# Windowed attention in a four-layer kernel: the softmax quotient moved to VectorE, one more gather issued by ScalarE, a shorter root and a bias sum placed by hand

## The chip, the core and the metric

The kernel runs on one core of a Trainium2 chip. A core has five engines with instruction streams of their own: TensorE (PE: matrix products into the accumulator memory PSUM; its weight loads are listed apart as PEld), VectorE (DVE), ScalarE (ACT), GpSimd (POOL) and SyncE (SP, which here issues transfers only). The metric is the time of the whole program on the device in microseconds. Three runs of the kernel before gave a median of 3369.8 us (3368.98 to 3379.31).

## The reference

The input is a batch of 8 images of 128 channels, 56 x 56 pixels, in fp32. Four residual layers follow one another, each on a group norm of its input (`x = x + layer(_gn(x))`). The change is in layer 0, attention between windows; one line of layer 1 moves.

```python
# layer 0, per image: 7 x 7 windows of 8 x 8 pixels, 8 heads of 16 channels
proj = xw @ W_qkv + b_qkv                      # queries, keys, values
logit = einsum('npc,nqc->npq', mean(q) * SCALE, mean(k))
topk_logit, r_idx = top_k(logit, 4)            # each window picks 4 windows
k_sel, v_sel = kv_pix[r_idx]                   # 256 keys and values a window
attn = softmax(einsum('bmqc,bmkc->bmqk', q_h * SCALE, k_sel))
o = einsum('bmqk,bmkc->bmqc', attn, v_sel)
out = (o + lepe) @ W_o + b_o                   # lepe: 3x3 depthwise of the values
```

Group norm takes `1 / sqrt(var + eps)` per group. Layer 1 is a recurrence over the 3136 pixels of an image, `h = tanh(xgate + h @ w_hh.T)`, where `xgate` has the two biases `b_ih + b_hh` added. Layers 2 and 3 are 3x3 convolutions.

## The kernel before

Layer 0 works on pairs of windows: 8 images of 49 windows make 196 pairs (`END`). A loop over p from -3 to END + 5 writes the order of TensorE, ScalarE, VectorE and GpSimd out by hand (`manual_schedule`); each engine executes its instructions in the order in which this loop emits them. SP's instructions are put into its queue in the order of their issue as well. In one turn, each step is a different stage of a different pair:

- `scores(p + 2)` (L534): queries times keys, 16 products into the four PSUM banks s0 to s3; `maxima` (L541, VectorE): the negated maxima of each bank; `halve` (L547, L548, GpSimd) splits them into two bf16 parts; `flip` (L553, TensorE) turns them; `flipped` (L557, ScalarE) copies them to SBUF as `nm`.
- `shifted(p + 1)`: four products of ones with `nm` start the banks t0 to t3 (L566), and 32 products of keys with queries are added (L576); `exponentials` (L586, ScalarE, one per bank) read them.
- `values(p)` (L600): 64 products of the gathered value pixels with the exponentials, into one bank `po`. The pixels carry columns of ones, so `po` holds for each group of 16 channels also the divisor of the softmax. TensorE first waits for the semaphores `landed`, which count the arrival of the pixels.
- then, for pair p: `divisors` (VectorE: a transpose of `po`, L622, which reads the whole bank; reciprocals of its divisors, L628; a transpose that spreads them back, L630), `first_heads` (ScalarE, L610: the even heads of `po` times a mask), `both_heads` (VectorE, L615: the odd heads added) and `divide` (GpSimd, L648: numerator times reciprocal, written into the strip `o` of a row of windows in image order).
- `join` (L437, GpSimd) adds `o` to the depthwise result `lep`; `project` multiplies by W_o, and VectorE adds it into X (L450).

Into the turns a planner places further jobs: for each strip of seven windows queries, keys, image, pixels, depthwise convolution and projection, and for each image the norm's statistics and the routing. A job has a TensorE part and an "end", the instruction that reads the PSUM result. Each turn has up to three jobs, `one`, `two` and `light`. The order of a turn is one of two strings, SHORT or LONGER (with a depthwise job, or with `two` alone). PSUM is shared by a table of slots: `values` uses bank s0 again, `one` t0, `two` t1, `flip` t2. So the next score product into s0 has to wait until all readers of `po` are done, and the next ones product into t1 until the end of `two` is. In SHORT the end of `two` comes last in the turn; it is on ScalarE except for projections. VectorE's own loose work (normalising, window sums, statistics) goes where a running `weight` per turn is smallest; the norm's ends and the routing aren't counted in that weight.

`fetch` (L515) issues the gathers of value pixels, two windows a turn and four transfers of 32 KB each: seven by SP and the first of each pair by ScalarE, all into a ring of six windows. The index of each comes from a register that `loaded` (L470) fills from the routing table in SBUF: SP for four windows at a time, ScalarE for every other window of seven.

For each image after the first, `var_end` takes the reciprocal root without ScalarE's table: a first value by integer arithmetic (L248 to L250) and three Newton steps of four VectorE instructions (L254 to L257). For layer 1, `bg = b_ih + b_hh` (L917) is written behind layer 0 in the program, and its place in VectorE's stream is left to the scheduler.

Of the kernel before, what the change touches and what calls it, by code (L numbers as in the profile page):

```python
# [11 lines left out]
F32 = mybir.dt.float32  # L12
# [34 lines left out]
def conv_stack_kernel(ctx: ExitStack, tc: tile.TileContext, a: dict, out: bass.AP):  # L47
# [76 lines left out]
    broken = keep.tile([1, 1], I32, name="broken")  # L124
    held = keep.tile([P, KH * (NCH - 1) * B // 16], F32, name="held")
    between = ExitStack()
    samp = between.enter_context(tc.tile_pool(name="samp", bufs=2))
    with ExitStack() as l0:
# [76 lines left out]
        def measure(b):  # L205
# [37 lines left out]
            def var_end():  # L243
# [9 lines left out]
                for _ in range(3):  # L253
                    nc.vector.tensor_tensor(t, y, y, ALU.mult)  # L254
                    nc.vector.tensor_tensor(t, t, v, ALU.mult)
                    nc.vector.tensor_scalar(t, t, -0.5, 1.5, ALU.mult, ALU.add)
                    nc.vector.tensor_tensor(y, y, t, ALU.mult)  # L257
# [175 lines left out]
        def join(b, i):  # L433

            o, t = os_.pop((b, i)), lepes[b, i]
            engine = nc.vector if (b, i) == (B - 1, NBLK - 1) else nc.gpsimd
            engine.tensor_add(t, t, o)  # L437
# [37 lines left out]
        def chosen(W, t, engine):  # L475

            if (engine, W, t) not in known:
                b, w = divmod(W, NWIN)
                if engine == mybir.EngineType.Activation:
                    at = selrs[b].rearrange("p (w t) -> p w t", t=TOPK)[:, w : min(w + 7, NWIN) : 2, t]  # L480
                    known.update(((engine, W + 2 * k, t), v) for k, v in enumerate(loaded(at, engine)))
# [25 lines left out]
        def fetch(W):  # L507

            for o in range(2):
                for t in range(TOPK):  # L510
                    h = (t % 2) * WPX
                    engine, kind = (nc.sync, mybir.EngineType.SP) if o or t else (
                        nc.scalar, mybir.EngineType.Activation)
                    at = chosen(W + o, t, kind)
                    dma = engine.dma_start(  # L515
                        ring[h : h + WPX, section(W + o, t // 2), :],
                        vpix[(W + o) // NWIN][bass.ds(at, 1)].rearrange("o x c -> (o x) c"),
                    )
                    dma.then_inc(landed[(W + o) % RING], 16)
                    tc.no_tile_sem_insts.add(dma.ins.name)  # L520
                    tc.add_to_no_dep_group(f"rows{W + o}", dma.ins)
# [66 lines left out]
        def values(p):  # L588
# [6 lines left out]
            for o in range(2):  # L595
                for h in range(2):
                    for c in range(2):
                        for g in range(4):
                            at = (section(2 * p + o, c) - h) * P + 2 * g + h
                            mm = nc.tensor.matmul(  # L600
                                po[g * CL : (g + 1) * CL, o, h], flat[:, at : at + 8 * CL - 7 : 8],
# [5 lines left out]
        def first_heads(p):  # L607

            v = pairs[p]["v"] = win.tile([P, 2, WPX], F32, name=f"v_{p}", tag="v", bufs=1)
            nc.scalar.activation(v, pairs[p]["po"][:, :, 0], AF.Identity, scale=hmask[:, 0:1])  # L610

        def both_heads(p):

            s_ = pairs[p]
            nc.vector.scalar_tensor_tensor(s_["v"], s_["po"][:, :, 1], hmask[:, 1:2], s_["v"], ALU.mult, ALU.add)  # L615

        def divisors(p):
# [3 lines left out]
            t = win.tile([P, 2, 2, 2, CL], F32, name=f"den_{p}", tag="den", bufs=1)  # L621
            nc.vector.transpose(  # L622
                t.rearrange("p o h b r -> p (o h b r)"), s_["po"].rearrange("p o h q -> p (o h q)")
            )
            at = t[:, 0, 0, 0, 16:17]
            den = bass.AP(at.tensor, at.offset, [list(at.ap[0]), [4 * CL, 2], [CL, 2], [2 * CL - 16, 2]])
            rden = win.tile([P, 2, 2, 2, 1], F32, name=f"rden_{p}", tag="rden", bufs=1)
            nc.vector.reciprocal(rden.rearrange("p o b h c -> p o b (h c)"), den)  # L628
# [5 lines left out]

        def divide(p):

            s_ = pairs.pop(p)
            for o in range(2):
                W = 2 * p + o
                b, w = divmod(W, NWIN)  # L640
# [1247 lines left out]
```

## Time and profile before

| | us |
|---|---|
| median of three runs | 3369.8 |
| the profiled execution | 3365.47 |
| its span, first to last instruction | 3363.6 |
| TensorE busy in it | 3246.4 |
| layer 0: first score product to the last value product | 29.4 to about 1187.8 |
| busy from 504 to 588 us (84 us): PE / PEld / DVE / ACT / POOL | 82.2 / 60.3 / 70.4 / 53.4 / 64.9 |
| busy from 1008 to 1092 us (84 us): PE / PEld / DVE / ACT / POOL | 77.2 / 54.3 / 56.0 / 48.6 / 59.4 |

The page gives the busy time of each engine, its course in 40 slices, the transfers, the chain of work that ended last, and the costliest groups. A row of a timeline is: start, duration, engine, line, operation, output <- inputs, shape and count, and in brackets the engine's idle time before it and what ended that. PE times are modelled in part, since products are pipelined: a TensorE that is held in the middle of a group can look busy. Engine names with a q (ACTq, SPq) are sequencer instructions such as the issue of a transfer. In the longest stretches of layer 0 a pair takes between 5.0 and 6.2 us.

### The profile page before, as it was taken

The page shows a single profiled execution, that of the slowest core. Times are in us where ns is not written, and L with a number is a line of the kernel's source. Part 1 is how long each engine was busy: PE and PEld are TensorE (multiplying, and loading weights), DVE is VectorE, ACT ScalarE, POOL GpSimd, SP SyncE. Part 2 cuts the span into 40 slices and gives each one's busy share as a digit, 9 for nine tenths or more (in the row PEclk, how much of TensorE's full clock was granted, in tenths as well). Part 3 has the DMA queues.
Part 4 walks back from the last instruction along what each step waited for, and adds up shares of the span by engine and source line. Part 5 has one row for each costly group of instructions (what it writes and reads, how often), then busy time and mean ns, then how long its engine had stood idle before and what let it go on. Part 6 is the DMA issues. An engine that isn't in the chain of part 4 may idle for free.

```text
span 3363.6 us, 103407 instructions
## 1 busy us (share of the span) xinstructions
PE 3246.4 (97%) x41152; PEld 2743.4 (82%) x41152; DVE 1767.8 (53%) x4066; ACT 1412.6 (42%) x2935; POOL 1291.8 (38%) x3797
## 2 busy tenths in 40 slices
PE   7999999999999899999999999999999999999998
PEld 5777767667676689999999999999999953489898
DVE  5888888788776732221111111111122247799999
ACT  4666666566665522222222222222211144455554
POOL 4777877877777721111111111111000046422221
PEclk9999999999999989999999999999999999999999
DMA  5455555545445411110000000000012146301001
GB/s 152 132 142 134 146 142 134 138 124 143 124 129 140 112 58 45 48 48 18 1 1 1 1 1 1 1 1 1 1 51 60 57 122 181 94 20 39 27 32 40
DMA packets 197564, 239.02 MB, mean 71 GB/s; under 512 B 42848, under 2 KB 150112, under 8 KB 197072
## 3 DMA queue, kind: packets, MB, share of 16 engines
q0 software_dynamic: 34624, 117.03, 12.7%
q1 hardware_dynamic: 145936, 108.38, 11.3%
q10 hardware_dynamic: 16512, 6.90, 0.9%
q8 instruction: 326, 5.34, 0.7%
q14 instruction: 166, 1.36, 0.1%
HBM read 133.64 MB, written 67.56 MB: 60 GB/s over the span
## 4 chain that ended last, share of the span: by engine, by line
PE 75%; DVE 18%; issue 3%; POOL 1%; ACT 1%; DMA 1%; SPq 0%; POOLq 0%; DVEq 0%; ACTq 0%
PE ps L1041 35%; PE s L534 6%; PE po L600 6%; PE po L1076 5%; PE plep L420 4%; PE pc L1267 4%; PE t L576 4%; DVE nmax L541 3%; PE pi L1016 3%; PE t L566 1%; PE pc L1275 1%; DVE u_pc3b L1632 1%; PE pq L390 1%; PE pvp L319 1%; DVE va L1499 1%
## 5 line engine op out<-in xcount | busy, mean ns | idle before, releaser
L1041 PE MATMUL ps<-hs,w_gates 128*128 128x136 f32 x7680 | 932.9, 280 | 0.4 <-issue 0.4
L1041 PEld LDWEIGHTS ps<-hs,w_gates 128*128 128x128 f32 x7680 | 911.1, 190 | 8.6 <-issue 0.5
L1064 ACT ACTIVATE hs<-ps,bg 128x136 f32<-128x136 f32 x744 | 237.9, 371 | 933.1 <-PE ps L1041 925.6
L586 ACT ACTIVATE e<-t 128x512 f32<-128x512 f32 x784 | 445.6, 595 | 345.3 <-PE t L576 273.6
L541 DVE TENSOR_REDUCE nmax<-s 128x2 f32<-128x512 f32 x784 | 487.0, 685 | 196.4 <-PE s L534 195.6
L1019 DVE SCALAR_TENSOR_TENSOR inp<-pi,bine,th 128x272 f32<-128x272 f32 x186 | 84.7, 496 | 889.2 <-ACT th L1018 889.2
L1005 POOL TENSOR_TENSOR xn<-X,ctr 128x136 f32<-128x136 f32 (+1 forms) x186 | 96.3, 536 | 876.4 <-PE pi L1016 871.6
L1041 PEld LDWEIGHTS ps<-inp,w_gates 128*128 128x128 f32 x2976 | 370.2, 190 | 13.5 <-PE pi L1016 1.1
L1041 PE MATMUL ps<-inp,w_gates 128*128 128x136 f32 x2976 | 375.4, 279 | 0.7 <-PE pi L1016 0.7
L496 POOL COPY ks<-kT 128x64 f32 x1568 | 297.0, 234 | 106.2 <-PE t L576 64.8
L600 PE MATMUL po<-e,ring 128*32 128x64 f32 x12544 | 247.2, 231 | 24.7 <-DVE nmax L541 17.9
L600 PEld LDWEIGHTS po<-e,ring 128*32 128x32 f32 x12544 | 220.0, 149 | 49.6 <-DVE nmax L541 20.1
L534 PE MATMUL s<-ks,qm 32*128 32x256 f32 x3136 | 228.4, 403 | 19.0 <-DVE v L615 15.2
L576 PE MATMUL t<-qm,ks 32*128 32x128 f32 x6272 | 235.6, 273 | 0.6 <-issue 0.6
L576 PEld LDWEIGHTS t<-qm,ks 32*128 32x128 f32 x6272 | 216.5, 188 | 4.8 <-issue 1.4
L1513 PE MATMUL pc3b<-vb,u_w2c_t 128*128 128x196 f32 x1152 | 200.9, 336 | 19.9 <-DVE vb L1494 19.9
L1513 PEld LDWEIGHTS pc3b<-vb,u_w2c_t 128*128 128x128 f32 x1152 | 197.3, 194 | 22.2 <-DVE vb L1494 22.0
L1076 PE MATMUL po<-hs,xw 128*128 128x272 f32 x744 | 203.9, 396 | 3.4
L1513 PE MATMUL pc3a<-va,u_w1c_t 128*128 128x196 f32 x1152 | 198.2, 332 | 9.1 <-DVE d_pc3a L1530 4.3
L1513 PEld LDWEIGHTS pc3a<-va,u_w1c_t 128*128 128x128 f32 x1152 | 192.9, 191 | 13.6 <-issue 10.2
L534 PEld LDWEIGHTS s<-ks,qm 32*128 32x128 f32 x3136 | 144.6, 185 | 50.1 <-DVE v L615 27.4
L1076 PEld LDWEIGHTS po<-hs,xw 128*128 128x128 f32 x744 | 132.0, 190 | 28.8 <-ACT hs L1068 9.1
(288 smaller groups left out, 4410.7 us busy)
## 6 DMA issues: line engine op xcount, KB each, us to landing
ring<-vpix SPq DMA_DIRECT2D x1372, 32.0 KB
v<-vimg POOLq DMA_DIRECT2D x56, 290.0 KB, 3.9
v<-vimg POOLq DMA_DIRECT2D x56, 289.5 KB, 4.8
v<-vimg POOLq DMA_DIRECT2D x56, 289.0 KB, 5.7
kept<-gk SPq DMA_DIRECT2D x56, 272.0 KB, 2.0
g<-kept SPq DMA_DIRECT2D x56, 272.0 KB, 2.6
xkeep<-X POOLq DMA_DIRECT2D x56, 224.0 KB, 2.5
vimg<-vrow POOLq DMA_DIRECT2D x54, 232.0 KB, 2.8
```

The lines of the kernel that those rows point to most:

```text
L420: nc.tensor.matmul(st["pl"][g * CL : (g + 1) * CL], wlep[:, dy, g, :], rows[:, g, dy : dy + WS, :HW], start=(dy == 0), stop=(dy == 2),)
L496: nc.gpsimd.tensor_copy(kw[:, t : t + 1, :], ks[b][:, bass.ds(at, 1), :])
L534: nc.tensor.matmul(s_["s"][g][:, o, :], w["qm"][h].rearrange("p h x -> p (h x)"), w["kw"][h], start=True, stop=True,)
L541: nc.vector.tensor_reduce(s_["nmax"][:, :, g], s_["s"][g], AX.X, ALU.max, negate=True)
L576: nc.tensor.matmul(s_["t"][g][:, o, c], w["kw"][h, c * P : (c + 1) * P], w["qm"][h].rearrange("p h x -> p (h x)"), start=False, stop=(o == ...
L586: nc.scalar.activation(s_["e"][g], s_["t"][g], AF.Exp)
L600: mm = nc.tensor.matmul(po[g * CL : (g + 1) * CL, o, h], flat[:, at : at + 8 * CL - 7 : 8], s_["e"][g][:, o, c, h * WPX : (h + 1) * WPX], ...
L1041: nc.tensor.matmul(ps[f][:, i], w, src, start=(i == 0 and k == 0 and h != fresh), stop=(k == KH - 1 if h else k == KI - 1 and (s < WARM or ...
L1064: nc.scalar.activation(hs[f][:, s % 2, i], ps[f][:, i], AF.Tanh, bias=bg[:, m : m + 1])
L1076: nc.tensor.matmul(po, wout[:, k, :], hs[k // 2][:, :, k % 2], start=(k == 0), stop=(k == KH - 1))
L1267: nc.tensor.matmul(pcs[n][r * CL : (r + 1) * CL], w3[:, dy, r, :], rows3[:, r, i * WS + dy : i * WS + dy + WS, :HW], start=(dy == 0), stop ...
L1513: nc.tensor.matmul(bank[:, half].rearrange("p (y x) -> p y x", x=H4), u[:, dy, k, :], v[:, k, i * RB + dy : i * RB + dy + RB, :], start=(d ...
```

## The change

The quotient is now taken between two transposes on VectorE, where the queries lie on the partitions: `turned` transposes `po`, and `divide` takes the reciprocals, multiplies numerators with them, and transposes the product into the strip `o`, which is now laid out window by window. `first_heads`, `both_heads` and GpSimd's product are gone; `join` reads `o` in the order of the image. Only `turned` reads `po`.

`fetch` takes one window. `fetch0` stands at the start of a turn, `fetch1` (the pair's second window) behind `flipped`, ahead of `lit`, the hooks, the tails and the last end. ScalarE issues the first gather of both windows, SP the other six; ScalarE's registers are loaded for eight successive windows.

The Newton steps become two instructions each (`scalar_tensor_tensor`) with one scaling at the end. The planner adds the norm's two ends, the means and the routing to the weight of the turns in which they stand. In LONGER turns the banks of `one` and `two` are exchanged. The bias sum `bg` is hooked to turn END // 2 + 10 of layer 0.

```diff
-                for _ in range(3):
-                    nc.vector.tensor_tensor(t, y, y, ALU.mult)
-                    nc.vector.tensor_tensor(t, t, v, ALU.mult)
-                    nc.vector.tensor_scalar(t, t, -0.5, 1.5, ALU.mult, ALU.add)
-                    nc.vector.tensor_tensor(y, y, t, ALU.mult)
+                for c in (3.0, 12.0, 768.0):
+                    nc.vector.scalar_tensor_tensor(t, y, v, y, ALU.mult, ALU.mult)
+                    nc.vector.scalar_tensor_tensor(y, t, -c, y, ALU.add, ALU.mult)
+                nc.vector.tensor_scalar(y, y, -1.0 / 8192, None, ALU.mult)
...
-            engine.tensor_add(t, t, o)
+            t = t.rearrange("p u (j v) -> p u j v", v=WS)
+            engine.tensor_add(t, t, o.rearrange("p j (u v) -> p u j v", v=WS))
...
-                    at = selrs[b].rearrange("p (w t) -> p w t", t=TOPK)[:, w : min(w + 7, NWIN) : 2, t]
-                    known.update(((engine, W + 2 * k, t), v) for k, v in enumerate(loaded(at, engine)))
+                    at = selrs[b].rearrange("p (w t) -> p w t", t=TOPK)[:, w : min(w + 8, NWIN), t]
+                    known.update(((engine, W + k, t), v) for k, v in enumerate(loaded(at, engine)))
...
-            for o in range(2):
-                for t in range(TOPK):
-                    h = (t % 2) * WPX
-                    engine, kind = (nc.sync, mybir.EngineType.SP) if o or t else (
-                        nc.scalar, mybir.EngineType.Activation)
+            for t in range(TOPK):
+                h = (t % 2) * WPX
+                engine, kind = (nc.sync, mybir.EngineType.SP) if t else (nc.scalar, mybir.EngineType.Activation)
...
-        def first_heads(p):
-            v = pairs[p]["v"] = win.tile([P, 2, WPX], F32, name=f"v_{p}", tag="v", bufs=1)
-            nc.scalar.activation(v, pairs[p]["po"][:, :, 0], AF.Identity, scale=hmask[:, 0:1])
-        def both_heads(p):
+        def turned(p):
             s_ = pairs[p]
-            nc.vector.scalar_tensor_tensor(s_["v"], s_["po"][:, :, 1], hmask[:, 1:2], s_["v"], ALU.mult, ALU.add)
+            t = s_["turned"] = win.tile([P, 2, 4, CL], F32, name=f"turned_{p}", tag="turned", bufs=1)
+            nc.vector.transpose(t.rearrange("p h k r -> p (h k r)"), s_["po"].rearrange("p h o q -> p (h o q)"))
...
         def divide(p):
+            t = pairs.pop(p)["turned"]
+            part, at = list(t.ap[0]), t.offset
+            den = bass.AP(t.tensor, at + 16, [part, [CL, 4], [4 * CL - 16, 2]])
+            rden = win.tile([P, 4, 2, 1], F32, name=f"rden_{p}", tag="rden", bufs=1)
+            nc.vector.reciprocal(rden.rearrange("p k h c -> p k (h c)"), den)
+            v = bass.AP(t.tensor, at, [part, [CL, 4], [4 * CL + 16, 2], [1, 16]])
+            ot = win.tile([P, 4, 2, 16], F32, name=f"ot_{p}", tag="ot", bufs=1)
+            nc.vector.tensor_tensor(ot, v, rden.broadcast_to((P, 4, 2, 16)), ALU.mult)
...
-                nc.gpsimd.tensor_tensor(
+                nc.vector.transpose(
+                    os_[b, i][:, j : j + n].rearrange("p o q -> p (o q)"),
+                    ot[:, 2 * o : 2 * o + 2 * n].rearrange("p k h r -> p (k h r)"),
                 )
...
+        for b, (name, n) in itertools.product(range(1, B), (("mean", 9), ("var", 13), ("means", 5), ("route", 10))):
+            weight[placed[name, b]] += n
...
+        hook(END // 2 + 10, lambda: nc.vector.tensor_add(bg, ih, hh))
...
-        SHORT = """fetch scores shifted gather max0 max1 values exp0 max2 exp1 max3 halve ahead one light two flip exp2
-            divisors first end1 exp3 flipped both divide lit hooks tails end2"""
-        LONGER = """fetch scores shifted gather max0 max1 values exp0 max2 exp1 max3 halve ahead two exp2 divisors first
-            flip light one exp3 flipped both divide lit hooks tails end2 end1"""
+        SHORT = """fetch0 scores shifted gather max0 max1 values exp0 max2 exp1 max3 halve ahead one light two flip exp2
+            root turned divide end1 exp3 flipped fetch1 lit hooks tails end2"""
+        LONGER = """fetch0 scores shifted gather max0 max1 values exp0 max2 exp1 max3 halve ahead two exp2 root turned
+            divide flip light one exp3 flipped fetch1 lit hooks tails end2 end1"""
...
+                    slot = dict(one="two", two="one").get(name, name) if longer else name
```

The order of TensorE's instructions is the same before and after; on ScalarE the second gather of a turn, with its register load where there is one, now stands between L557 and the last end.

## The prediction

> **What bounds the kernel now.** I read the page first. Its slices show three stages: layer 0 with its attention in the first 14 slices (to about 1190 us), layer 1's recurrence, then layers 2 and 3. TensorE is busy 97% of the span, and the change touches layer 0 and one line at layer 1's start.
>
> ```profile
> span 3363.6 us, 103407 instructions
> PE 3246.4 (97%) x41152; PEld 2743.4 (82%) x41152; DVE 1767.8 (53%) x4066; ACT 1412.6 (42%) x2935; POOL 1291.8 (38%) x3797
> ```
>
> Second, the waits between 60 and 1060 us, layer 0's steady part:
>
> ```profile
> PEld s L534 <- DVE v L615: 17.6, 48, 0.6
> ...
> PEld po L600 <- DVE nmax L541: 17.1, 9, 4.2
> ...
> PEld L566 <- issue: 39.2, 126, 0.5
> ...
> DVE bg L917 <- DMA vecs<-in_L_conv_b_hh_dram: 5.6, 1, 5.6
> ...
> PE po L600 <- DMA ring<-vpix: 4.1, 1, 4.1
> ```
>
> The reader should see three waits of TensorE on VectorE or a transfer (L534, L600), and one that names nobody: 126 pauses of up to 0.5 us before the ones-weights of L566. The timeline says who that is. One pair of windows at 401.59 us:
>
> ```profile
> 401.59 1.15 PE L534 MATMUL s<-ks,qm 32*128 32x256 f32 x16
> ...
> 401.84 0.37 ACT L557 COPY nm<-flip 128x256 bf16<-128x256 bf16 x1
> 401.92 0.48 ACTq L515 DMA_DIRECT2D ring<-vpix  x1
> 402.10 0.71 ACT L307 ACTIVATE vrow<-pvt,bqkv 128x448 f32<-128x448 f32 x1
> 402.34 0.10 PEld L566 LDWEIGHTS <-ones 2*128 2x128 bf16 x2
> ...
> 402.86 0.10 PEld L566 LDWEIGHTS <-ones 2*128 2x128 bf16 x2 [0.42 <-issue]
> ...
> 404.07 1.15 PE L600 MATMUL po<-e,ring 128*32 128x64 f32 x57
> ```
>
> ScalarE empties bank t1 (L307, "end2" of this pair's second job) until 402.81; TensorE's second ones product, which refills t1, starts at 402.86. I cut the timeline at each pair's first score product and count from there. The second ones product starts at 0.97 at the earliest (49 pairs), otherwise 0.05 behind the end of end2; values begins 1.22 later in every group: 2.19 for 0.97, 2.34 for 1.12 (59 pairs), 2.55 for 1.33 (11 pairs). So each 0.1 us that end2 slips is 0.1 us of TensorE, already now. Over the 180 pairs that matter below, the mean start is 1.12.
>
> Third, ScalarE alone at 368 us:
>
> ```profile
> 368.34 0.37 ACT L557 COPY nm<-flip 128x256 bf16<-128x256 bf16 x1 [1.07 <-PE flip L553]
> 368.61 0.64 ACT L427 ACTIVATE lep<-plep,lbv 128x448 f32<-128x448 f32 x1
> 370.34 0.48 ACTq L515 DMA_DIRECT2D ring<-vpix  x1
> 370.86 1.58 ACT L586 ACTIVATE e<-t 128x512 f32<-128x512 f32 x3 [1.62 <-PE t L576]
> ```
>
> Here a register load of 1.48 us stood before the gather's issue, and the exponential, which in other pairs starts at 2.32, started 0.04 after that issue ended, at 2.66. ScalarE's next instruction waits behind an issue.
>
> **The change, part by part** (against the profiled execution, 3365.5 us with a span of 3363.6; the median of the runs shown is 3369.8, 4.3 above).
>
> *Two gathers by ScalarE: the cost.* SP issues 6 instead of 7 per pair, each 0.65 us apart. ScalarE issues 2, and the new one (fetch1) stands behind L557 and ahead of end2; the first stays behind end2. One issue is two register steps and the 0.48 us of the row above, 0.61 together. end2 now starts about 0.27 behind the start of L557 (368.34, 368.61); with the issue between them 0.03 + 0.61 + 0.04 = 0.68 behind. L557 starts at 0.16 in an undisturbed pair, and end2 takes 0.60 to 0.71, say 0.64: it ends at 0.16 + 0.68 + 0.64 = 1.48, and TensorE's refill starts at 1.53 instead of 1.12. That is +0.41 to 0.42 in 180 pairs (the changed order has no end2 behind fetch1 in 15 of the others), 76 us. ScalarE also reads indices from SBUF once per eight windows; for odd images that load now falls on fetch1. In the changed order 24 pairs have load, issue, end2. The loads have a median of 0.92, a mean of 1.05 and a maximum of 1.82 us: 24 x 1.07 = 26 us. Sum **+102 us**. Ends: were only the 0.48 us instruction in the way, 0.28 x 180 + 24 x 0.6 = 65; did the issue wait for the copy's end as well, 0.75 x 180 + 24 x 1.5 = 171. I take 0.41, since the row at 370.86 shows exactly issue end + 0.04. Behind end2 wait the other gather's issue and the exponentials; these have till 2.7 and lose nothing further. The swap of t0 and t1 in pairs with a depthwise job changes only which ones product waits.
>
> [...]
>
> *Quotient by VectorE.* Out: transpose of po 0.45, reciprocal 0.20, transpose back 0.31, both-heads 0.31 on VectorE; 0.37 on ScalarE; 0.47 on GpSimd. In: the same transpose, reciprocal, a 128x128 product, a transpose back. The product is between a 128x1 operation (0.16) and GpSimd's neighbour row on VectorE (L1009, two 128x136 in 1.09: 0.54); nearest is both-heads of the same size, 0.31. VectorE's load stays: 766 us busy in the 960 from 100 to 1060, 4.67 per pair of 5.75 or more. What moves is the release of bank s0: after the first transpose, not after four instructions and often the projection's 0.64 (L450). Score products wait for v 55 times in layer 0, 16.8 us by the same cut: gone, because the transpose ends near 4.2 and the next scores come after 5.1. GpSimd loses 0.47 per pair; its join reads o in strips of eight instead of rows, between 1.13 (no change) and twice that, once in 3.5 pairs, inside 4.7 busy us per pair. The four late flips that wait for GpSimd and the one at 73 us, 4.5 us, go with it. At the last pair the join no longer waits for GpSimd and L450: 1 us.
>
> *Root and planner.* The Newton chain is 15 instructions, 418.36 to 421.80 us; now 10, about 2 us. The planner now counts statistics and routing, so the sums and statistics of 0.6 us that stood directly behind the root go elsewhere. In the changed order the worst VectorE groups fall from 7.9 to 5.8 us by these durations. Each image's root held values (L600) 1.1 to 2.2 us: the nine waits above.
>
> *Bias sum.* It stood where VectorE reached it before its vector had landed:
>
> ```profile
> 645.22 0.61 DVE L213 BATCH_NORM_STATS2 st<-X 128x6 f32<-128x448 f32 x1
> 651.45 0.16 DVE L917 TENSOR_TENSOR bg<-vecs 128x4 f32<-128x4 f32 x1 [5.62 <-DMA vecs<-in_L_conv_b_hh_dram]
> ```
>
> That pair lasted 11.65 us instead of 5.66. Now the sum stands some five pairs later, 25 us after the landing: no wait.
>
> All L600 waits but the first pair's sum to 20.5 us; the pairs around them lost 5.3 more (at 419 us 9.17 with 2.19 idle, against some 6.0 for its kind). SP's lighter queue should hide most of the 4.1 us behind the weight transfers, though these now follow each other directly: I count it fully and keep 4 us for the range. Gains: 16.8 + 25.8 + 4.5 + 1 = **48 us**.
>
> Sum: 102 - 48 = **+54 us**; 3365.5 + 54 = 3419.5 for a profiled execution, 3369.8 + 54 = **3424** for the median.
>
> **Rivals.**
> - *Faster: end2 doesn't slip.* If ScalarE's issue runs beside its compute, the gains stand alone: 3369.8 - 48 = 3322. It decides where the slip costs less than 48 us, 0.27 us a pair. For it: in the row at 401.92 the issue overlaps the copy; against it: 370.86.
> - *The holds let the clock fall.* The L600 stalls over 2 us cost about 1 us beyond their idle time, those of 1.2 nothing. With load and slip the 24 long holds come to 1.5 to 2.2 us: at 1 us each +24, 3448. [...]
> - *VectorE becomes the bound.* With products at 0.54 and slowed transposes it would need 5.2 us per pair, still under 5.75; only over 6.2 would scores wait again. Each 0.2 us beyond costs 39 us: 3463.
> - *The gains don't come*, because scores then wait for something else: 3369.8 + 102 - 17 (v kept) to - 48: up to 3441.
>
> **How the numbers follow.** Slip with gains 0.66; clock falls too 0.10; VectorE bound 0.05; part of the gains 0.07; no slip, faster, 0.09; about no change 0.03. Range: the slip's lower end, 65 - 48, gives 3387, and the clock and VectorE cases reach 3463; the full 171 would be 3493 and is left out with the faster case. So 3385 to 3463. A measurement here tells 0.3% (10 us) from no change: faster 0.09, same 0.03, slower 0.88.
>
> **What would show it.** Right: the second ones product near 1.53 in plain pairs, 2.6 where a load precedes; a TensorE pause before it named by a ScalarE evacuation; no wait on v, none of 1 to 4 us at L600; the bias sum without a wait; SP with idle time. Wrong: end2 still 0.27 behind the copy, or scores waiting for the new transpose. The largest risk is an issue on ScalarE that isn't in the way of the evacuation.

## The result and the profile after

The changed kernel takes 3465.95 us (median, 3463.26 to 3469.94) against 3370.65 us before (six executions each), ratio 1.028 with a 95% interval of 1.0267 to 1.0293: **95 us slower**, where the prediction said 54 slower and a range up to 3463. The direction and the place are as forecast; the size is not.

The page of the changed kernel, its first lines and the groups that answer to those of before (a group's last column is the idle time ahead of it and what ended most of that):

```profile
span 3467.9 us, 102912 instructions
...
PE 3295.5 (95%) x41152; PEld 2760.2 (80%) x41152; DVE 1799.4 (52%) x4059; ACT 1362.3 (39%) x2739; POOL 1215.9 (35%) x3573
...
L599 PE MATMUL po<-e,ring 128*32 128x64 f32 x12544 | 258.9, 239 | 4.7 <-DMA ring<-vpix 3.8
...
L533 PE MATMUL s<-ks,qm 32*128 32x256 f32 x3136 | 232.0, 402 | 2.3 <-ACT vp L342 2.1
...
L565 PE MATMUL t<-nm,ones 2*128 2x512 bf16 x784 | 125.5, 385 | 89.3 <-ACT lep L427 36.7
```

The same two groups on the page of before:

```profile
L600 PE MATMUL po<-e,ring 128*32 128x64 f32 x12544 | 247.2, 231 | 24.7 <-DVE nmax L541 17.9
...
L534 PE MATMUL s<-ks,qm 32*128 32x256 f32 x3136 | 228.4, 403 | 19.0 <-DVE v L615 15.2
```

The waits that the change was to remove are gone: the values (now L599) have 4.7 us of idle ahead of them instead of 24.7, the scores (L533) 2.3 instead of 19.0, and of both about 1 us is left on VectorE. (The profiled execution took 3469.94 us, 104.5 more than the profiled one of before; the medians are 95 apart.) A new one of 89.3 us stands ahead of the ones products (L565). TensorE's own busy time also rose, from 3246.4 to 3295.5 us, with the same 41152 products, at a granted clock of 0.979 in the mean of the execution instead of 0.988.

The waits of the same stretch as before, 60 to 1060 us (total, times, longest, in us):

```profile
PEld L565 <- issue: 138.5, 153, 3.3
...
PE t L565 <- ACT lep L427: 29.0, 41, 2.8
ACT lep L427 <- issue: 26.6, 43, 2.7
...
PE t L565 <- ACT vrow L307: 17.4, 43, 2.8
```

The pauses ahead of the ones-weights grew from 39.2 us, the longest 0.5, to 138.5, the longest 3.3. Most of them end with an evacuation by ScalarE (L427, L307), and ahead of these ScalarE is idle itself, most of it put down to "issue" (26.6 us at L427, 12.0 at L307): time in which the profile shows nothing that it waits for. The timeline shows what that is, first in a pair with a register load, then in the pair after it, without one (start and length in us, engine, line):

```profile
538.75 1.15 PE L533 MATMUL s<-ks,qm 32*128 32x256 f32 x16
538.91 0.37 ACT L556 COPY nm<-flip 128x256 bf16<-128x256 bf16 x1 [1.40 <-PE flip L552]
...
541.22 0.49 ACTq L514 DMA_DIRECT2D ring<-vpix  x1
541.76 0.63 ACT L427 ACTIVATE lep<-plep,lbv 128x448 f32<-128x448 f32 x1 [2.48 <-issue]
...
542.44 0.40 PE L565 MATMUL t<-nm,ones 2*128 2x512 bf16 x4 [2.55 <-ACT lep L427]
...
548.06 1.15 PE L533 MATMUL s<-ks,qm 32*128 32x256 f32 x16
548.22 0.37 ACT L556 COPY nm<-flip 128x256 bf16<-128x256 bf16 x1 [1.08 <-PE flip L552]
548.36 0.48 ACTq L514 DMA_DIRECT2D ring<-vpix  x1
...
548.89 0.69 ACT L307 ACTIVATE vrow<-pvt,bqkv 128x448 f32<-128x448 f32 x1 [0.30 <-issue]
...
549.63 0.39 PE L565 MATMUL t<-nm,ones 2*128 2x512 bf16 x3 [0.23 <-ACT vrow L307]
```

In the second pair everything is as the prediction worked it out: copy at 0.16 from the pair's start, issue, evacuation 0.67 behind the copy (forecast 0.68), the ones product behind it at 1.57 (forecast 1.53; the median over all pairs is 1.52). In the first, the copy is followed by a gap of 1.94 us, from 539.28 to the issue at 541.22; the register load, 2.10 us from 538.92, stands in it. TensorE is idle for 2.55 us, and this pair takes 9.3 us, 3.5 more than the next.

The load itself, by its line (shortest / median / longest in ns; first the kernel before, then the changed one):

```profile
L470 SPq TENSOR_LOAD <-selr x104: 298/973/1483, 29.9 to 1180.0; - x104
L470 ACTq TENSOR_LOAD <-selr x52: 284/920/1822, 43.2 to 1155.4; - x52
```

```profile
L471 SPq TENSOR_LOAD <-selr x104: 296/973/1601, 30.2 to 1280.3; - x104
L471 ACTq TENSOR_LOAD <-selr x56: 281/1730/3006, 42.9 to 1284.7; - x56
```

There were 52 loads and there are 56, but ScalarE's median went from 0.92 to 1.73 us. The prediction counted how often a load stands in the way and took its length from the trace before. But in the diff the slice changes too, from every second window of seven (four values) to eight windows (eight values).

What a long load does to the clock is seen by cutting stretches out of layer 0 (length; busy time of each engine; the granted clock is the first number behind POOL's count). The changed kernel, the pair with the load at 538.5, the one after it, and one at 509.1:

```profile
core 0: us, PE busy (x) PEld busy (x) DVE busy (x) ACT busy (x) POOL busy (x), PEclk, DMA share, GB/s
...
538.50:547.80 9.30, 6.75 (x126) 4.97 (x123) 4.57 (x10) 3.18 (x6) 4.81 (x16) 0.82 0.34 98
547.80:553.60 5.80, 5.57 (x123) 3.90 (x122) 4.58 (x9) 3.21 (x6) 3.86 (x15) 1.00 0.91 207
...
509.10:520.70 11.60, 9.15 (x145) 5.57 (x143) 5.26 (x11) 3.68 (x8) 4.92 (x19) 0.71 0.34 107
```

The granted clock is 1.00 in the plain pair and 0.82 and 0.71 in the pairs with a long load. So a hold costs its idle time and then a slow stretch: (1 - 0.82) x 9.3 = 1.7 us and (1 - 0.71) x 11.6 = 3.4 us. 21 pairs behind 60 us have over 1 us of idle ahead of the second ones product, 48.6 us in all. In 20 of them the clock fell, which cost 1.7 us in 16 and about 3.4 in four, 41 us by this reckoning.

The length of a hold alone does not decide this. In the records of the granted clock in the two traces, before and changed kernel, the 32 stretches at a lowered clock within layer 0 (8 and 24) are 3.41 us long or 6.83, all at 0.50, and within a trace they start whole multiples of 3.41 us apart. Three steps of that length around the first pair above (same columns):

```profile
539.80:543.21 3.41, 0.86 (x28) 0.77 (x27) 2.49 (x4) 0.63 (x1) 0.00 (x0) 1.00 0.21 56
543.21:546.62 3.41, 3.41 (x85) 2.80 (x78) 0.49 (x2) 1.66 (x4) 2.67 (x9) 0.50 0.08 21
546.62:550.04 3.42, 3.19 (x35) 1.81 (x37) 2.61 (x7) 1.57 (x4) 2.31 (x8) 1.00 1.00 216
```

In the first step TensorE is idle for 2.55 us, in the second the clock is halved. Over these two traces (layer 0 from 60 us on, steps at full clock) the next step was a lowered one after all 27 steps with 1.64 us of idle or more (6 before, 21 in the changed kernel), after neither of two with 1.52 and 1.60, and after one of 626 with less than 1.3 (1.21 us, at 1283.9 in the changed kernel). A lowered step that itself had 0.53 us of idle or more (six cases) was followed by another lowered one, one without idle (28 cases) was not: hence the cost of 1.7 us or of 3.4. So what tells the holds apart here is how much of one falls into one step. The one of the 21 that lowered nothing is 2.17 us long and lies 0.65 in one step and 1.52 in the next (1171.27 to 1174.68 us, and from there to 1178.09).

The stage of layer 0, from the first score products to the last, before and after, is then

```profile
30.00:1172.50 1142.50, 1091.16 (x25006) 785.99 (x24998) 891.87 (x2001) 697.76 (x1428) 871.50 (x2975) 0.99 0.51 133
```

```profile
30.00:1279.90 1249.90, 1142.42 (x25010) 801.96 (x25003) 923.00 (x1992) 648.37 (x1234) 796.73 (x2757) 0.96 0.47 122
```

Of 107.4 us more, 51.3 is TensorE busy longer with the same work and 56.1 is idle: 87.7 of waits of the ones products for ScalarE's evacuations, less 31.6 for all other waits. By the clock's records the lowered clock took 49.5 us of this stage, against 15.4 before, so 34 of the 51.3; the other 17 are not explained. (Some of it may be waiting too, which was not shown: at 525.42 us of the trace before, four ones products stand as 0.69 us of unbroken work although the ones-weights wait 0.42 us inside it; four at 542.44 above take 0.40.) Layers 1 to 3 differ by 3 us.

### The profile page after: what moved, and what is told of

It is laid out like the page before. It is cut to its first block, busy times and chain, and to the rows that moved or that the text cites. A ratio compares the mean times of both kernels' runs of the same rounds, so it can differ in the third digit from the quotient of the medians.

```text
span 3467.9 us, 102912 instructions
## 1 busy us (share of the span) xinstructions
PE 3295.5 (95%) x41152; PEld 2760.2 (80%) x41152; DVE 1799.4 (52%) x4059; ACT 1362.3 (39%) x2739; POOL 1215.9 (35%) x3573
## 3 DMA queue, kind: packets, MB, share of 16 engines
q0 software_dynamic: 34624, 117.03, 12.5%
## 4 chain that ended last, share of the span: by engine, by line
PE 73%; DVE 12%; ACT 6%; issue 4%; ACTq 4%; DMA 1%; POOL 0%; DVEq 0%; SPq 0%; POOLq 0%
PE ps L1028 34%; PE po L599 7%; PE po L1063 5%; PE t L575 5%; PE pc L1254 4%; PE plep L420 4%; ACTq L514 3%; PE pi L1003 2%; PE t L565 2%; PE pq L390 2%; PE py L446 1%; PE pc L1262 1%; PE pc3b L1500 1%; PE pvp L319 1%; ACTq L471 1%
## 5 line engine op out<-in xcount | busy, mean ns | idle before, releaser
L585 ACT ACTIVATE e<-t 128x512 f32<-128x512 f32 x784 | 431.0, 596 | 348.0 <-PE t L575 268.9
L599 PE MATMUL po<-e,ring 128*32 128x64 f32 x12544 | 258.9, 239 | 4.7 <-DMA ring<-vpix 3.8
L599 PEld LDWEIGHTS po<-e,ring 128*32 128x32 f32 x12544 | 229.8, 151 | 30.8 <-issue 8.3
L575 PE MATMUL t<-qm,ks 32*128 32x128 f32 x6272 | 248.1, 280 | 2.1 <-issue 2.0
L533 PE MATMUL s<-ks,qm 32*128 32x256 f32 x3136 | 232.0, 402 | 2.3 <-ACT vp L342 2.1
L565 PE MATMUL t<-nm,ones 2*128 2x512 bf16 x784 | 125.5, 385 | 89.3 <-ACT lep L427 36.7
L1500 PEld LDWEIGHTS pc3a<-va,u_w1c_t 128*128 128x128 f32 x1152 | 195.0, 193 | 11.6 <-issue 9.4
L565 PEld LDWEIGHTS <-ones 2*128 2x128 bf16 x784 | 36.9, 92 | 169.8 <-issue 165.6
```

The costliest lines, as they stand in the source:

```text
L533: nc.tensor.matmul(s_["s"][g][:, o, :], w["qm"][h].rearrange("p h x -> p (h x)"), w["kw"][h], start=True, stop=True,)
L565: nc.tensor.matmul(s_["t"][g], ones[r], s_["nm"][r].rearrange("p (o c) q -> p o c q", c=1).broadcast_to((2, 2, 2, P)), start=True, stop=Fa ...
L575: nc.tensor.matmul(s_["t"][g][:, o, c], w["kw"][h, c * P : (c + 1) * P], w["qm"][h].rearrange("p h x -> p (h x)"), start=False, stop=(o == ...
L585: nc.scalar.activation(s_["e"][g], s_["t"][g], AF.Exp)
L599: mm = nc.tensor.matmul(po[g * CL : (g + 1) * CL, h, o], flat[:, at : at + 8 * CL - 7 : 8], s_["e"][g][:, o, c, h * WPX : (h + 1) * WPX], ...
L1500: nc.tensor.matmul(bank[:, half].rearrange("p (y x) -> p y x", x=H4), u[:, dy, k, :], v[:, k, i * RB + dy : i * RB + dy + RB, :], start=(d ...
```

## The experiments

The theory, after the result: ScalarE's fetch1 holds the evacuation; in plain pairs by its issue, in some 24 pairs by a long load as well, after which TensorE's clock falls; the gains of the other parts are there underneath. Rivals: that VectorE's quotient is on the path, that a hold costs its length and no more, that the gains were never there.

**The second fetch behind the last evacuation.**

```diff
 SHORT
-            root turned divide end1 exp3 flipped fetch1 lit hooks tails end2"""
+            root turned divide end1 exp3 flipped lit hooks tails end2 fetch1"""
 LONGER
-            divide flip light one exp3 flipped fetch1 lit hooks tails end2 end1"""
+            divide flip light one exp3 flipped lit hooks tails end2 end1 fetch1"""
```

> The changed kernel with the second window's fetch issued behind ScalarE's last evacuation of the pair instead of between the two. Theory (the hold): what costs is that the address steps, the index load and the issue of this fetch keep ScalarE from the second evacuation, for which the next pair's second ones product waits. Behind the last evacuation nothing of the pair waits for them, so the second ones product should start within 1.2 us of the pair's start in plain pairs (1.53 in the changed kernel), load pairs should have no 9 to 12 us lengths, and the 143 us of holds should go while the gains of 48 us stay: 3370 - 48 = 3322 us; if the loads of 1.73 us then make the next pair's first exponential late by up to 0.6 us in some 48 pairs, up to 3350. Rival (VectorE's quotient on the path, or the clock lower for another cause): the time stays within 15 us of the changed kernel's 3466.

Measured 3360.08 us, ratio to before 0.9968 (0.9953 to 0.9983). 106 us of the changed kernel are gone by moving one step, so the rival that puts the loss on VectorE falls. But the time is 10 us above the upper end of the theory. Its waits, 60 to 1160 us, have no more holds at L565, but others:

```profile
PE pq L390 <- ACT e L585: 9.3, 16, 1.1
PE plep L420 <- ACT e L585: 8.7, 11, 1.9
PE py L446 <- ACT e L585: 5.7, 8, 1.2
```

Behind the last evacuation stand the next pair's exponentials. Load (1.74 us in the median here), issue, and the next pair's issue (0.48 each) together take longer than their slack; every such wait in the pairs, with smaller ones of the same kind, comes to some 29 us.

**Loads of four values instead of eight, in the place of the change.**

```diff
-                    at = selrs[b].rearrange("p (w t) -> p w t", t=TOPK)[:, w : min(w + 8, NWIN), t]
+                    at = selrs[b].rearrange("p (w t) -> p w t", t=TOPK)[:, w : min(w + 4, NWIN), t]
```

> The changed kernel with ScalarE's index loads cut from eight strided values to four, so twice as many loads of about 0.9 us (the median of the four-value loads before) instead of 1.73; all else as changed. The sum of the load times is about the same: 48 x 0.9 = 43 us against 24 x 1.73 = 42. Theory (a long hold costs more than its length, since the clock falls in it and the next pairs run slower): shorter holds cost only their length, so 30 us are saved: about 3436, and the mean granted clock rises from 0.979 to 0.983 or more. Rival (a hold costs its length and no more): within 8 us of the changed kernel, 3458 to 3474, since the same time is only cut up differently.

Measured 3446.46 us, between the two forecasts. The clock of the whole run rose from 0.979 to 0.986 as the theory had it, and the stage shows which half came true:

```profile
30.00:1259.40 1229.40, 1120.11 (x25010) 788.02 (x25006) 922.88 (x1992) 650.64 (x1234) 793.02 (x2756) 0.98 0.47 124
```

TensorE's idle time is 109.3 us against 107.5: twice as many loads (104) of half the length (median 0.90) cost the same idle time, as the rival said. The busy time fell by 22.3 us, and the granted clock accounts for it: over the whole spans (0.986 of 3445.4 us, 0.979 of 3467.9) the lowered clock took 48.2 us against 72.8, some 25 less. Why not all of it came back is seen in single pairs of this kernel:

```profile
285.70:293.10 7.40, 6.21 (x144) 3.79 (x143) 5.58 (x12) 3.23 (x6) 3.68 (x14) 1.00 0.29 96
...
557.30:565.80 8.50, 6.97 (x133) 5.84 (x132) 4.42 (x11) 3.29 (x7) 4.54 (x17) 0.80 0.32 96
...
814.20:822.30 8.10, 6.17 (x144) 3.70 (x142) 5.12 (x11) 3.54 (x7) 4.45 (x18) 1.00 0.34 113
```

TensorE's idle time is 1.19 us in the first, 1.53 in the second, 1.93 in the third; only the second shows a lowered clock (0.80). Of the 40 pairs of this kernel with over 1 us of idle time and a load, cut out in the same way, none of the 16 under 1.3 us shows a lowered clock, 8 of 21 between 1.3 and 2.0 do (0.77 to 0.82), and 2 of 3 over 2. Each fall cost about 1.7 us, 17 us in all, against 41 in the changed kernel.

**Neighbouring values.** ScalarE's indices are copied into a tile of their own, so that its load of eight reads eight words in a row; one small transfer more per sample. The fetch stays where the change put it.

```diff
                 nc.sync.dma_start(selrs[b], sel)
+                firsts[b] = samp.tile([1, NWIN], I32, name=f"first_{b}", tag="first")
+                nc.sync.dma_start(firsts[b], sel[:, 0:1])
...
-                    at = selrs[b].rearrange("p (w t) -> p w t", t=TOPK)[:, w : min(w + 8, NWIN), t]
+                    at = firsts[b][:, w : min(w + 8, NWIN)]
```

> The changed kernel, with the fetch's second half where the change puts it, but ScalarE's indices (the first choice of every window) also copied to a tile of their own, one behind the other, so that its load of eight reads neighbouring values; one more small transfer per sample on SP's queue. Theory (the price is of the stride, about 0.2 us a value, and neighbours cost far less, as SP's 16 in 0.97 us): a load of eight takes 0.5 to 0.7 us instead of 1.73, the holds with a load shrink by over 1 us and the clock recovers: 3405 to 3430 us. Rival (ScalarE pays 0.2 us for each value however they lie): the load stays at 1.7 us and the time at 3458 to 3474.

Measured 3401.80 us, ratio 1.0095 (1.0078 to 1.0112), just under the theory's 3405 to 3430: 64 us less than the changed kernel, for the layout of eight integers. The load and the stage:

```profile
L473 ACTq TENSOR_LOAD <-first x56: 288/553/1061, 45.5 to 1217.3; - x56
```

```profile
29.50:1212.50 1183.00, 1109.72 (x25014) 780.23 (x25014) 923.84 (x1992) 651.31 (x1234) 794.75 (x2758) 0.99 0.50 129
```

The load takes 0.55 us instead of 1.73 for the same eight values. 24 loads shorter by 1.18 us make 28 us; the clock accounts for most of the rest: of ten pairs cut out with over 1 us of idle time only one shows a lowered clock here (0.79 over 8.2 us: 1.7 us, against 41), and busy time fell by 32.7.

**Both.** The two edits together, fetch1 behind the last evacuation and its indices as neighbours.

> Both: the second window's fetch behind the last evacuation, and ScalarE's indices as neighbours in a tile of their own. Theory: a load of 0.5 to 0.7 us behind the last evacuation is hidden before the next pair's first exponential, the 29 us of waits at fills fall under 5, and the gains stay: 3332 us (3322 to 3342). Rival (not the loads but the two issues of 0.5 us made the first exponential late, or the time returns in another wait): 3354 or more.

Measured 3333.49 us, ratio to before **0.9892** (0.9876 to 0.9909): the fastest kernel of this study, 36 us under before and inside the theory's 3322 to 3342. Waits, 60 to 1060 us, and the stage:

```profile
PE po L601 <- DVE nmax L542: 4.8, 9, 0.7
PE t L577 <- issue: 4.5, 7, 1.0
```

```profile
29.60:1148.70 1119.10, 1091.34 (x25010) 782.66 (x25010) 933.67 (x1992) 633.53 (x1234) 791.65 (x2757) 0.99 0.53 136
```

TensorE is busy as long as before the change, and idle for 27.8 us of the stage instead of 51.3. (That is 23.4 of the 36 us. Layers 1 to 3 are 6 us shorter in this trace; the rest is that the traced execution of before was 4 us under its median here and this one 2.5 over.)

**Late, with loads of four strided values.** The first two edits together.

> The second window's fetch behind ScalarE's last evacuation, and ScalarE's index loads of four strided values instead of eight. With the loads of eight this placing took 3360 us, and its trace shows some 29 us in which TensorE waits at a fill, because the next pair's first exponential came late behind the loads of 1.73 us. Theory (only what of a load goes past a slack of about one us is paid): loads of 0.9 us are hidden nearly always, 29 us fall to 5: 3336 us (3328 to 3346). Rival (the load time is paid in full, wherever it is cut): twice as many loads of half the length leave it at 3354 to 3366.

Measured 3337.53 us (0.9909, 0.9892 to 0.9925). The theory holds: loads of 0.90 us, twice as many, hide behind the slack before the first exponential where 1.74 us did not. Here cutting a load up did pay: of TensorE's waits for the exponentials (9.3, 8.7 and 5.7 us with loads of eight) the largest left is 1.6 us.

**The second fetch ahead of the copy of the maxima**, with neighbouring indices.

```diff
-            root turned divide end1 exp3 flipped fetch1 lit hooks tails end2"""
+            root turned divide end1 exp3 fetch1 flipped lit hooks tails end2"""
```

(and the same in LONGER.)

> ScalarE's indices as neighbours, and the second window's fetch placed between the last exponential and the copy of the flipped maxima, where ScalarE waits for TensorE (118 us in 115 waits, about 1 us each). Theory (the wait hides about 1 us of issue): plain pairs cost nothing and pairs with a load 0.5 us each: 3335 to 3350. Rival (the copy of the maxima comes late, and with it the second ones product and the clock): 3375 or more.

Measured 3335.10 us (0.9900, 0.9880 to 0.9919), within the theory's range and not distinguishable from the best. With neighbouring indices the second fetch stood as well on either side of the copy and last evacuation (3335.10 and 3333.49 us), and cost 66 to 68 us between them (3401.80).

**Only the gathers, as the change has them, on the kernel before.** Fetch in two halves, eight strided values, fetch1 between the last two evacuations; quotient, root and bias sum as before.

```diff
...
-            divisors first end1 exp3 flipped both divide lit hooks tails end2"""
+            divisors first end1 exp3 flipped fetch1 both divide lit hooks tails end2"""
...
```

> The kernel before with only the change of the gathers: the fetch in two halves, ScalarE issuing the first gather of each window, its loads of eight strided values, the second half between its two last evacuations. Quotient, root and bias sum as before. Theory (holds and gains add): 3370 + 143 = 3513 us, less what of the 17 us of waits for v and the 26 us of product stalls comes from SP's queue and is relieved by the gather that SP loses: 3470 to 3515. Rival (the hold hurts only because the new quotient takes the slack of the pair's end): within 40 us of before, under 3410.

Measured 3487.28 us (1.0344, 1.0326 to 1.0363), as expected: this part alone costs 115 us, more than the whole change.

**Everything but the gathers.** The changed kernel with one fetch per pair, seven gathers by SP and one by ScalarE.

```diff
-            for t in range(TOPK):
-                engine, kind = (nc.sync, mybir.EngineType.SP) if t else (nc.scalar, mybir.EngineType.Activation)
+            for o in range(2):
+                for t in range(TOPK):
+                    engine, kind = (nc.sync, mybir.EngineType.SP) if o or t else (
+                        nc.scalar, mybir.EngineType.Activation)
...
-            root turned divide end1 exp3 flipped fetch1 lit hooks tails end2"""
+            root turned divide end1 exp3 flipped lit hooks tails end2"""
```

> The changed kernel with the fetch as it was before: one fetch per pair, seven gathers issued by SP and one by ScalarE, loads of four strided values. Quotient on VectorE between the turns, shorter root and placed bias sum stay. Theory (the loss is all of the second gather on ScalarE): 3370 less the gains of 48 us, less those that belong to the gathers (the waits for v, 17 us): 3322 to 3340. Rival (the quotient between the turns lengthens the chain on VectorE and TensorE waits for it): 3390 or more.

Measured 3364.00 us (0.9974, 0.9959 to 0.9990): not 3322 to 3340, nor the rival's 3390. Where the gain went is in its waits, 60 to 1160 us:

```profile
PE po L601 <- DMA ring<-vpix: 21.9, 14, 4.7
PE po L601 <- DVE nmax L542: 5.2, 10, 1.0
```

The scores wait for v no more. In the kernel before, the same view has

```profile
PE po L600 <- DVE nmax L541: 16.4, 12, 4.0
...
PE po L600 <- DMA ring<-vpix: 4.1, 1, 4.1
```

The product's waits for VectorE fell from 16.4 to 5.2 us, but those for the fetched rows are 21.9 instead of 4.1. In the kernel called "both" above, which differs from this one in the gathers alone (six a pair by SP instead of seven), they are at most 0.3: the next bound lay with the gathers, seven of them in SP's queue.

**The shorter root alone (with the planner's count), and the bias sum alone, on the kernel before.**

```diff
-                for _ in range(3):
-                    nc.vector.tensor_tensor(t, y, y, ALU.mult)
-                    nc.vector.tensor_tensor(t, t, v, ALU.mult)
-                    nc.vector.tensor_scalar(t, t, -0.5, 1.5, ALU.mult, ALU.add)
-                    nc.vector.tensor_tensor(y, y, t, ALU.mult)
+                for c in (3.0, 12.0, 768.0):
+                    nc.vector.scalar_tensor_tensor(t, y, v, y, ALU.mult, ALU.mult)
+                    nc.vector.scalar_tensor_tensor(y, t, -c, y, ALU.add, ALU.mult)
+                nc.vector.tensor_scalar(y, y, -1.0 / 8192, None, ALU.mult)
...
+            weight[placed[name, b]] += n
```

> The kernel before with only the shorter root (10 instructions instead of 15) and the planner counting statistics and routing. The prediction gave it the nine waits of 1.1 to 2.2 us at the product: some 12 us, 3358. Against it: with root, quotient and bias sum changed and the gathers as before, the product still waited 27 us and the time was 3364, so what ended these waits last may be the fetched rows: then 3364 to 3372.

```diff
+        hook(END // 2 + 10, lambda: nc.vector.tensor_add(bg, ih, hh))
...
-        nc.vector.tensor_add(bg, bih, bhh)
```

> The kernel before with only the bias sum of layer 1 placed some pairs later. The prediction: the pair of 11.65 us becomes one of about 5.7, 6 us saved, 3364. Rival (the product of that pair waits for fetched rows behind the weight transfers on SP's queue, whatever VectorE does): within 2 us of before.

Measured 3371.45 us (ratio 0.9989, 0.9972 to 1.0005) and 3372.25 us (0.9986, 0.9973 to 0.9999), against 3373.49 before. By these intervals the root's 12 us did not come (at most 9); the bias sum's 6 us are not excluded (0 to 9). The waits, 60 to 1160 us, of the root alone, then of the bias sum alone:

```profile
PE po L599 <- DMA ring<-vpix: 20.3, 12, 4.1
...
PE po L599 <- DVE nmax L540: 4.9, 7, 2.1
```

```profile
PE po L601 <- DMA ring<-vpix: 16.2, 9, 4.1
...
PE po L601 <- DVE nmax L542: 10.6, 7, 2.2
```

VectorE's waits at the product shrink as forecast (from 16.4 to 4.9 and 10.6), and with the bias sum moved its pair took 6.03 us instead of 11.65, with no wait of its product: the rival's number came, not its mechanism. The rows' waits are 12 to 16 us more than in the trace of before, but at other pairs: with the root alone those over 1 us stand at 391, 473, 481, 988, 1032, 1077 and 1160 us, where VectorE had held nothing. What changed there is SP's lead. The last gather of a pair was issued 7.8 us ahead of its product in the kernel before (median over the pairs), 7.1 and 6.7 in these two, 6.6 in everything but the gathers, and 12.2 where SP has six gathers. That SP's queue takes back what VectorE gives is argued from this and not shown: in the bias run one of the rows' waits (2.7 us at 501) stands ahead of the first turn in which that run does anything else, and the one trace of the kernel before took 8 us less than the median measured beside these runs.

**The gathers alone, in their good form, on the kernel before**: fetch1 behind the last evacuation, neighbouring indices, and nothing else of the change.

> The kernel before with only the gathers changed, in their good form: ScalarE issues the first gather of each window, the second behind its last evacuation, its indices lie as neighbours. Quotient, root and bias sum as before. Theory (a gather that leaves SP takes away the waits of the product for the fetched rows, about 20 us of idle and 5 of clock, and the waits of the scores for v, 17 us, stay): 3345 us (3338 to 3354). Rival (the gain of 36 us needs the quotient between the turns too, since the next wait stands right behind): 3358 or more.

Measured 3357.58 us, ratio 0.9941 (0.9923 to 0.9960), 16 us less than before by the medians and 20 by the ratio; between the theory's 3354 and the rival's 3358, almost the rival's. Its waits, 60 to 1160 us:

```profile
PE s L534 <- DVE v L615: 14.5, 40, 1.0
PE po L600 <- DVE nmax L541: 13.8, 9, 2.6
```

The mirror of the runs before: now the rows are there in time, and VectorE's waits at the product remain.

By medians the gathers in good form are worth 16 us alone, all else 8 us alone, both together 36, 12 more than the two; by the ratios it is 20, 9 and 36, 8 more. Each of the three is good to some 5 or 6 us, so the surplus to about 10: that the parts are worth more together than alone is not clear of noise. And the hold, from the best kernel to the changed one, is 3465.95 - 3333.49 = 132.5 us; less 16 to 20 this gives 113 to 117 for the gathers alone as the change has them, where 115 were measured.

How SP's queue stands is in its own waits, 100 to 1100 us, before and in the best kernel:

```profile
SPq L515 <- PE po L600: 31.1, 63, 2.7
```

```profile
SPq L516 <- PE po L601: 162.3, 146, 2.6
```

Before, SP waited 31 us for the product to free the ring, in 63 of some 170 pairs. With six gathers it waits 162 us, in 146 pairs: it now has time to spare.

## Why the prediction was wrong

By medians, in the prediction's own terms:

| step | predicted | measured | from |
|---|---|---|---|
| slip by the issue, with loads of 0.55 us | 76 + 24 x 0.55 = 89 | 68.3 | 3401.80 - 3333.49 |
| the rest of the loads | 24 x (1.07 - 0.55) = 12.5 | 64.2 | 3465.95 - 3401.80 |
| gains | -48 | -36.0 | 3333.49 - 3369.49 |
| sum | +54 | +96.5 | measured directly: +95.3 |

The kernel with neighbouring indices has one small transfer more per sample, and the runs come from different chips, so single terms are good to a few us.

**The step that failed is "24 x 1.07 = 26 us", the index loads ahead of the issue.** What the loads cost beyond 0.55 us each was 64.2 us where the prediction has 12.5. Two things were wrong with it. The length was taken from loads of four values, and the diff makes them eight: 1.73 us in the median instead of 0.92 (the prediction's 1.07 goes by their mean, 1.05), and the holds 1.9 to 3.4 us long instead of 1.5 to 2.2. And such a hold was counted at its length. In the changed kernel, where it is 1.9 us or more, it lowered the granted clock in 20 of 21 pairs, which cost 41 us more: each fall lasted 3.41 us or twice that at 0.50 of the clock, which loses 1.7 or 3.4. The prediction had this as a rival, "the holds let the clock fall", with a chance of 0.10 and 24 us; it was part of the main case, and 1.7 times as dear.

**The slip** was right in mechanism and place: evacuation 0.67 behind the copy for 0.68, ones product at a median of 1.52 for 1.53. What it cost was nearer the lower end that the prediction kept (65 us) than the 76 it took: "each 0.1 us that end2 slips is 0.1 us of TensorE" was somewhat too dear: between the kernels with neighbouring values, late and not, the second ones product moves by 0.43 us in the mean and the values by 0.34.

**The quotient.** Its waits went as forecast: 16.8 us of the scores for v are none. The product on VectorE takes 0.43 us on the mean where 0.31 was taken, and VectorE is busy for 923 us of the stage instead of 892; both lie beside TensorE. The rival "VectorE becomes the bound" has nothing for it. The forecast that the late flips go was wrong: the flip waited 2.8 us in 3 cases for GpSimd's halves before, 4.7 in 6 in the best kernel (60 to 1160 us).

**Root, bias sum and SP.** The whole change did remove the waits at the product (24.7 to 4.7), but the prediction gave nearly all of it to VectorE's parts, and SP's lighter queue a share behind the weight transfers only. The runs show that without SP's lighter queue the rows' waits stay at 16 to 22 us, and that the root alone gains less than 9. The "nine waits" that the prediction gave to the roots include the 4 us of the bias sum; the six at the images' roots come to 9.5. The sum was less wrong than its parts: 36 of 48 us. The bias sum itself has no wait any more (0.15 us at 755.1).

The faster rival, an issue that does not hold ScalarE's compute, is excluded by 115 us of the gathers alone. In the rival "the gains don't come" the sum is wrong as written: 102 - 17 gives 3455; its 3441 takes off 31, the gains without the 17 of v.

## What to carry to other kernels

Count a register load by its values and their stride, and read the diff's slices for it: eight values took 1.73 us here with one in every four words and 0.55 side by side, and the 0.92 of four in the trace before was no length for eight. An issue on ScalarE held the evacuation behind it, 0.67 behind the copy instead of 0.27, and with a load of eight TensorE was held for 1.9 to 3.4 us: put it, with its load, where nothing that TensorE waits for stands directly behind it (that alone gave 106 us here). When a wait is taken away, ask which queue then has less lead: with everything but the gathers, the product's waits for VectorE went from 16.4 to 5.2 us, those for the fetched rows from 4.1 to 21.9, at other pairs.

## What the runs showed of the hardware

- A register load (TENSOR_LOAD in the traces) of eight values, one in every four words, took ScalarE 1.73 us in the median (changed kernel), four such values 0.90 (loads of four), four with one in every eight words 0.92 (before), one value 0.28 (the eight shortest loads of the changed kernel, at the ends of the images); eight neighbouring ones 0.55 (neighbouring values), and SP's sixteen neighbouring ones 0.97 (before). An estimate from these medians: about 0.21 us for each further strided value ((1.73 - 0.28) / 7) and 0.04 for a neighbouring one ((0.55 - 0.28) / 7).
- Of the pairs cut out with a load and over 1 us of idle TensorE, none of 20 with 1.0 to 1.3 us shows a lowered granted clock (16 with the loads of four, 4 with neighbours), 8 of 25 with 1.3 to 1.8 do (the same two kernels), and 23 of 26 above that (the changed kernel and the loads of four), at 0.68 to 0.84 in the mean of the pair. Each fall cost about 1.7 us of TensorE's time or twice that. In layer 0 of the traces of before and of the changed kernel, from 60 us on and in steps of 3.41 us at full clock, the next step ran at 0.50 of the clock after all 27 steps with 1.64 us of idle TensorE or more, after neither of two with 1.52 and 1.60, after one of 626 with less than 1.3.
